# A memset of one element in a run of four indirect gathers, and gathers asked for two groups further on, in a message-passing kernel on one Trainium2 core

## The chip, the cores and the metric

The kernel runs on one core of one Trainium2 chip. The metric is device time in microseconds of one execution; the median of several runs is compared. One further execution was taken by the hardware profiler, and every row of a profile below is from such an execution.

## The reference

A graph has 6250 nodes of 128 features and 100000 edges, sorted by destination. For each edge the features of its source and of its destination go through three layers; the messages are averaged at the destination; a node update with a residual and a layer norm follows.

```python
msg_in = jnp.concatenate([node_features[row], node_features[col]], axis=-1)
h = jax.nn.relu(msg_in @ Wm1 + bm1)
h = jax.nn.relu(h @ Wm2 + bm2)
messages = h @ Wm3 + bm3
agg = jax.ops.segment_sum(messages, col, num_segments=num_nodes)
...
agg = agg / jnp.clip(count, 1.0)[:, None]
node_in = jnp.concatenate([node_features, agg], axis=-1)
upd = jax.nn.relu(node_in @ Wn1 + bn1) @ Wn2 + bn2
return node_features + upd
```

## The kernel before

The first layer is split by its two inputs. In a prologue of about 45 us the kernel turns x, multiplies it by both halves of Wm1 and writes two tables to DRAM: one row of 256 numbers for each node as a source (atab, 1 KB a row) and one for each node as a destination (btab, as three bf16 terms). The edges are then worked through in 196 groups of 512 (four tiles of 128 edges). A group passes these stages:

- Gather (L527 to L536): GpSimd issues four indirect DMAs, one for each tile. Each fetches 128 rows of atab, by 128 indices that lie in SBUF, into one quarter of the tile `rows`. The four are called a run here. Four buffers of `rows` take turns, so the run of group i may only start when the transposes of group i-4 have read that buffer. Groups 0 and 1 take their first layer from other tiles, so group 2 is the first with a run.
- Transposes (`open_layer`, L558 to L572): sixteen products on TensorE turn the gathered rows into PSUM, with the identity as the moving operand. L582 adds the destination's terms by a one-hot product, and ACT adds the bias and cuts at zero (L588).
- Second layer (L596): sixteen fp32 products of 128x256 a group; DVE takes the maximum with the negative bias (L598).
- Sums (L604 to L624): a one-hot product sums the edges of a window of nodes; ACT copies the sums (L609), TensorE turns them (L617) and DVE adds them into an accumulator in SBUF (L624).
- From about the middle on the node update of finished nodes is interleaved.

One loop over steps k (L845 to L920) sets the order: step k does the first layer of group k, asks for a gather, does the second layer of group k-1, and then sums. TensorE, ACT and DVE run in the order in which this code is written. The order on GpSimd and SP is set by a scheduler at build time, from the code and its dependences. In this loop the gather of group k+2 is asked for in step k (L879, L880).

The indices: `sources(g)` (L749) hands a gather its indices. Those of even groups, and of groups up to 4, are read from `srcT` in place. Those of odd groups above 4 are first copied, 128x4 integers, into one of four slots of `srcP`. The copy is made by DVE in every second step for the group five ahead (L893), and for group 5 by ACT in step 2 (L878). Such a gather waits for its copy.

Of the kernel before, what the change touches and what calls it, by code (L numbers as in the profile page):

```python
# [10 lines left out]
F32 = mybir.dt.float32  # L11
# [9 lines left out]
P = 128  # L21
# [8 lines left out]
XS = 1  # L30
B_FIRST = 4
B_EARLY = 8
B_FROM = 10


@with_exitstack
def kernel(
# [36 lines left out]
    nc = tc.nc  # L74
# [4 lines left out]
    GT = 4  # L79
    GE = GT * P  # L80
    HE = 2 * P
    NG = -(-E // GE)
# [27 lines left out]
    const = ctx.enter_context(tc.tile_pool(name="const", bufs=1))  # L110
    dram = ctx.enter_context(tc.tile_pool(name="dram", bufs=1, space=DRAM))

    srcT = const.tile([P, NG, GT], I32, name="srcT")
    srcX = const.tile([P, 2 * XS, GT], I32, name="srcX")
    srcP = const.tile([P, 4, GT], I32, name="srcP")
# [19 lines left out]
    nc.vector.memset(idle, 0.0)  # L135
    ident = const.tile([P, P], F32, name="ident")
    make_identity(nc, ident)
    iota_n = const.tile([P, 1, WN], F32, name="iota_n")
    nc.gpsimd.iota(iota_n, pattern=[[0, 1], [1, WN]], base=0, channel_multiplier=0,
                   allow_small_or_imprecise_dtypes=True)  # L140
# [148 lines left out]
    halves = [slice(h * NQ, (h + 1) * NQ) for h in range(2)]  # L289
# [9 lines left out]
    with tc.tile_pool(name="prep", bufs=1) as prep, tc.tile_pool(name="pp", bufs=3, space=PSUM) as pp, tc.tile_pool(  # L299
        name="pb", bufs=5, space=PSUM  # L300
# [177 lines left out]
        for i in range(BLOCKS):  # L478
            tiles = range(4 * i, min(4 * i + 4, NT), 2)
            rows = a_rows[i % len(a_rows)]  # L480
# [34 lines left out]
    with edge, tc.tile_pool(name="wk", bufs=2) as wk, tc.tile_pool(  # L515
        name="banks", bufs=7, space=PSUM
# [7 lines left out]
        def bank():  # L524
            return banks.tile([P, 2, H], F32, name="bank")
# [1 line left out]
        def flat_bank():  # L527
            return bank().rearrange("p t h -> p (t h)")

        def gather(idx):  # L530
            ag = ld.tile([P, GT, H], F32, name="rows")
            for j in range(GT):
                nc.gpsimd.indirect_dma_start(  # L533
                    out=ag[:, j, :], out_offset=None, in_=atab[:, :],
                    in_offset=bass.IndirectOffsetOnAxis(ap=idx[:, j:j + 1], axis=0))
            return ag  # L536
# [21 lines left out]
        def open_layer(ag, nt, xt=None):  # L558
            nh = nt // 2
            ph = [bank() for _ in range(nh)]  # L560
            for c in range(HC):
                if xt is not None:
                    for h in range(nh):
                        nc.tensor.matmul(ph[h][:, c, :], w1[:, 0, c * P:(c + 1) * P], xt[:, h * HE:(h + 1) * HE],
                                         start=(c == 0), stop=False, skip_group_check=True)
                    continue
                for u in range(GT):
                    for h in range(nh):
                        nc.tensor.matmul(ph[h][:, c, u * NQ:(u + 1) * NQ], ag[halves[h], u, c * P:(c + 1) * P],  # L569
                                         ident[halves[h], halves[h]], is_transpose=True,  # L570
                                         start=(c == 0 and u == 0), stop=False, skip_group_check=True)
            return ph  # L572

# [63 lines left out]
        def nk_of(g):  # L637
            return 1 if g < 2 * HALVES or g >= GL else 2
# [108 lines left out]
            nc.sync.dma_start(rows_of(out, k), y[:r, :n, :])  # L747

        def sources(g):  # L749
            return srcP[:, g % 4, :] if g > 4 and g % 2 else srcT[:, g, :]  # L750

        def pace(g):
            return srcP[:, g % 4, :], srcT[:, g, :]
# [26 lines left out]

        B_STEPS = B_FROM + 2 * (NT - B_EARLY) + 2
        begins, step = {}, B_STEPS
# [5 lines left out]
        nodes, terms, rows = [], {}, {}  # L788
# [58 lines left out]
        def next_rows():  # L847
            for last in (False, True):
                for parts in next_four:
                    b_term(*parts, last)  # L850
# [6 lines left out]
        for g in range(-4, NG + 14, 2):  # L857
# [10 lines left out]
            for k in (g, g + 1):  # L868
                if k < NG:
                    s = st[k] = {}  # L870
                    if k == 1:
                        xts[1] = open_layer(None, NTS[1], xts[1])
                    s["h1"] = first_layer(rows.pop(k, None), terms.pop(k), ohts[k // 2][:, k % 2], NTS[k], nk_of(k),
                                          xts.pop(k, None))
                    if k == 0:
                        next_rows()
                    if k == 2:
                        nc.scalar.copy(*pace(5))  # L878
                if 2 * XS <= k + 2 < NG:  # L879
                    rows[k + 2] = gather(sources(k + 2))  # L880
                if k % 2 == 0 and k + 2 < NG:
                    make_hot(k // 2 + 1)
                if 0 <= k - 1 < NG:
                    second_layer(st.pop(k - 1)["h1"], h2s[(k - 1) % len(h2s)], NTS[k - 1])
                if k < NG:
                    node_step(k)
                if k <= NG:
                    turn_sums(k)
                some_sums(k)
                if k > NG:  # L890
                    turn_sums(k)
                if k % 2 == 0 and 2 <= k and k + 5 < NG:
                    nc.vector.tensor_copy(*pace(k + 5))  # L893
                if k >= NG:
                    node_step(k)
            if g < 6:
                clear(8)
            if g == 0:
                more_rows()
            t0 = B_EARLY + (g - B_FROM) // 2  # L900
            if g >= B_FROM and (g - B_FROM) % 4 == 0 and t0 < NT:
                pbt = bank()
# [21 lines left out]
        with tc.If(again > 0, preferred_fallthrough_block=True, label="again"):  # L924
            with tc.For_i(0, NG, 1) as g:
# [13 lines left out]
                with tc.For_i(0, more, 1):  # L939
                    idx = wk.tile([P, GT], I32, name="idx")  # L940
# [52 lines left out]
```

## Time and profile before

| | us |
|---|---|
| median of 3 runs | 1339.38 |
| lowest and highest run | 1335.79, 1342.36 |
| profiled execution, its time | 1338.36 |
| profiled execution, span from first to last instruction | 1336.6 |
| TensorE products busy | 1236.1 (92%) |
| TensorE weight loads busy (beside products) | 925.5 (69%) |
| GpSimd busy | 748.7 (56%) |
| DVE busy | 618.2 (46%) |
| ACT busy | 441.9 (33%) |
| granted TensorE clock, mean over the span | 0.981 |

In the rows of the profile PE is TensorE, PEld its weight loads, POOL GpSimd, DVE VectorE, ACT ScalarE, SP SyncE. A row of a time-line has the start and the length in us, the engine, the line of the kernel, what is written and read, how many alike follow each other, and in brackets the idle time of the engine just before and what ended it; "issue" means that nothing which the profile shows was waited for. A row of groups has the busy time in us, the mean length of one in ns, and the idle time before all of them. On GpSimd a gather's length is that of issuing it; its data moves afterwards.

### The profile page before, as it was taken

What the parts mean: (1) busy time and instruction counts of PE and PEld (TensorE: products, weight loads), DVE (VectorE), ACT (ScalarE), POOL (GpSimd) and SP (SyncE); (2) the same over time, 40 slices, a digit from 0 to 9 for tenths busy, and PEclk for the clock granted to TensorE, in tenths of its full rate; (3) what the DMA queues carried; (4) which work ended last, traced back from release to release, by engine and by line L of the source; (5) the groups of instructions that cost most, each with busy time, mean ns of one, the idle gap of its engine ahead of it and who ended that gap; (6) DMA issues with size and microseconds to landing.
All of it is one profiled execution on the core that took longest, in us unless ns stands there. A gap on an engine that the chain in (4) does not pass through costs nothing.

```text
span 1336.6 us, 27771 instructions
## 1 busy us (share of the span) xinstructions
PE 1236.1 (92%) x10031; PEld 925.5 (69%) x10032; DVE 618.2 (46%) x1551; ACT 441.9 (33%) x1102; POOL 748.7 (56%) x795
## 2 busy tenths in 40 slices
PE   9779998998999999999899999999999999999997
PEld 7556666666666666676677777777777777777675
DVE  6443333433334333434466554444445556556553
ACT  4432323323323323333333423333233333333331
POOL 2366665665665666656555465565655555555550
PEclk9879999999999999999999999999999999999998
DMA  8544434444434434434444344444444434443330
GB/s 287 177 125 134 132 108 127 130 115 129 133 106 128 135 107 125 134 106 131 126 118 119 114 125 128 118 120 129 118 118 118 115 109 118 109 123 110 106 91 4
DMA packets 107617, 163.90 MB, mean 123 GB/s; under 512 B 26367, under 2 KB 71549, under 8 KB 107457
## 3 DMA queue, kind: packets, MB, share of 16 engines
q0 software_dynamic: 37504, 102.29, 27.7%
q1 hardware_dynamic: 69425, 59.50, 14.0%
q8 instruction: 82, 1.34, 0.4%
q14 instruction: 62, 0.51, 0.1%
q10 hardware_dynamic: 544, 0.26, 0.1%
HBM read 142.48 MB, written 19.86 MB: 121 GB/s over the span
## 4 chain that ended last, share of the span: by engine, by line
PE 89%; issue 7%; DVE 2%; another core or an unknown queue 1%; DMA 1%; ACT 0%; SPq 0%; DVEq 0%
PE bank L596 54%; PE bank L569 9%; PE sum_bank L604 9%; PE bank L582 4%; PE bank L617 2%; PE pbt L431 2%; PE bank L727 2%; PE bank L700 2%; PE bank L719 2%; PE bank L715 2%; PE bank L904 1%; PE pt L448 0%; DVE acc L660 0%; DVE x_sb L598 0%
## 5 line engine op out<-in xcount | busy, mean ns | idle before, releaser
L596 PE MATMUL bank<-w,h 128*128 128x256 f32 x3128 | 768.7, 392 | 67.2 <-issue 64.6
L596 PEld LDWEIGHTS bank<-w,h 128*128 128x128 f32 x3128 | 581.7, 192 | 212.3 <-issue 131.1
L533 POOL DMA_INDIRECT rows<-atab,srcT x392 | 374.9, 956 | 260.6 <-issue 90.4
L533 POOL DMA_INDIRECT rows<-atab,srcP x384 | 364.2, 949 | 277.9 <-issue 126.5
L588 ACT ACTIVATE h<-bank,b 128x256 f32<-128x256 f32 x782 | 306.5, 476 | 395.6 <-remote 189.3
L598 DVE TENSOR_TENSOR x_sb<-bank,nb 128x512 f32<-128x512 f32 x263 | 181.0, 691 | 401.7 <-PE bank L596 233.7
L598 DVE TENSOR_TENSOR h_more<-bank,nb 128x512 f32<-128x512 f32 x128 | 88.3, 692 | 177.5 <-PE bank L596 75.0
L569 PEld LDWEIGHTS bank<-ident,rows 64*128 64x128 f32 x3096 | 112.7, 140 | 77.7 <-issue 56.8
L569 PE MATMUL bank<-ident,rows 64*128 64x64 f32 x3096 | 139.3, 230 | 0.0
L624 DVE TENSOR_TENSOR acc<-acc,bank 128x96 f32 x382 | 96.7, 253 | 51.7 <-PE bank L569 16.5
L604 PE MATMUL sum_bank<-x_sb,oh 128*32 128x257 f32 x1044 | 104.1, 393 | 3.0 <-issue 1.6
L609 ACT COPY part<-sum_bank 128x257 f32<-128x257 f32 x96 | 35.8, 373 | 197.0 <-PE bank L582 75.4
L582 PE MATMUL bank<-oht,terms 64*128 64x128 bf16 (+1 forms) x1132 | 82.6, 237 | 14.5 <-issue 10.9
L604 PE MATMUL sum_bank<-h_more,oh 128*32 128x257 f32 x512 | 59.1, 391 | 1.2 <-DVE h_more L598 0.6
L604 PEld LDWEIGHTS sum_bank<-x_sb,oh 128*32 128x32 f32 x1044 | 28.1, 108 | 41.7 <-issue 34.1
L582 PEld LDWEIGHTS <-terms 64*128 64x128 bf16 x1132 | 44.1, 97 | 16.1 <-issue 13.8
L617 PE MATMUL bank<-ident,part 128*128 128x128 f32 (+1 forms) x291 | 47.3, 271 | 0.5 <-ACT part L609 0.5
L745 ACT ACTIVATE y<-y,sh,rs 128x128 f32<-128x128 f32 (+3 forms) x50 | 22.1, 487 | 67.0 <-DVE sh L743 26.6
L695 DVE RECIPROCAL x_sb<-x_sb 128x256 f32<-128x256 f32 (+3 forms) x26 | 43.0, 1655 | 0.9
L617 PEld LDWEIGHTS bank<-ident,part 128*128 128x128 f32 (+1 forms) x291 | 36.6, 139 | 9.3 <-ACT part L609 1.0
L552 DVE TENSOR_TENSOR oh<-iota_n,dloc 128x256 f32<-128x256 f32 x98 | 40.8, 417 | 3.6 <-ACT dloc L838 3.6
L737 ACT ACTIVATE sd<-mv,eps 128x2 f32<-128x2 f32 (+3 forms) x26 | 7.7, 295 | 97.6 <-DVE mv L735 49.5
(157 smaller groups left out, 625.0 us busy)
## 6 DMA issues: line engine op xcount, KB each, us to landing
terms<-btab SPq DMA_DIRECT2D x566, 32.0 KB
places<-reltab SPq DMA_DIRECT2D x98, 128.0 KB
btab<-x_sb SPq DMA_DIRECT2D x10, 768.0 KB
rows<-atab,srcT POOLq DMA_INDIRECT x392
atab<-acc SPq DMA_DIRECT2D x12, 512.0 KB
rows<-atab,srcP POOLq DMA_INDIRECT x384
xr<-in_x_dram SPq DMA_DIRECT2D x23, 128.0 KB
out_dram<-y SPq DMA_DIRECT2D x23, 128.0 KB
```

The source lines that it names most:

```text
L533: nc.gpsimd.indirect_dma_start(out=ag[:, j, :], out_offset=None, in_=atab[:, :], in_offset=bass.IndirectOffsetOnAxis(ap=idx[:, j:j + 1], a ...
L552: nc.vector.tensor_tensor(oh[:, :ng].rearrange("p g j n -> p (g j) n"), iota.to_broadcast([P, ng * GT, WN]), dl.rearrange("p (j o) -> p j ...
L569: nc.tensor.matmul(ph[h][:, c, u * NQ:(u + 1) * NQ], ag[halves[h], u, c * P:(c + 1) * P], ident[halves[h], halves[h]], is_transpose=True, ...
L582: nc.tensor.matmul(ph[h][:, c, k * n:(k + 1) * n], bw[halves[h], k, c * P:(c + 1) * P], oht[halves[h], k * n:(k + 1) * n], start=False, st ...
L588: nc.scalar.activation(h1[:, c, h * HE:(h + 1) * HE], ph[h][:, c, :], AF.Relu, bias=b1[:, c:c + 1])
L596: nc.tensor.matmul(ph2[:, j - j0, :], h1[:, c, j * P:(j + 1) * P], w2[:, c, :], start=(c == 0), stop=(c == HC - 1))
L598: nc.vector.tensor_tensor(h2[:, j0:j0 + 2, :H], ph2, nb2.to_broadcast([P, 2, H]), op=ALU.max)
L604: nc.tensor.matmul(pg[w * WN:(w + 1) * WN, :H + 1], oh, h2, start=(t == 0), stop=(t == total - 1), skip_group_check=True)
L609: nc.scalar.copy(part[:nw * WN], pg[:nw * WN, :H + 1])
L617: nc.tensor.matmul(pt[:, c, :q], rows, ident[:q, :q], is_transpose=True, start=True, stop=True, skip_group_check=True)
L624: nc.vector.tensor_add(window, window, pt[:, :, j * WN:(j + 1) * WN])
L695: nc.vector.reciprocal(rc, rc)
```

## The change

1. A second tile `turner`, 128x128, is filled in the prologue by a copy of the identity on DVE. The sixteen transposes of a group read it in place of the identity; all other users keep the identity.
2. For groups from 20 on the source has, between the second and the third gather of a run, a memset on GpSimd that writes 1.0 to the one element [0, 0] of `turner`, which is 1.0 already.
3. Step k asks for the gather of group k+4 in place of k+2; steps 0 and 1 ask for two groups each (2 and 3, 4 and 5).
4. Group 5's indices are read in place, and the copy of ACT is gone; copied indices begin with group 7.

```diff
+GATED = 20
...
     ident = const.tile([P, P], F32, name="ident")
     make_identity(nc, ident)
+    turner = const.tile([P, P], F32, name="turner")
+    nc.vector.tensor_copy(turner, ident)
...
-        def gather(idx):
+        def gather(idx, gated=False):
             ag = ld.tile([P, GT, H], F32, name="rows")
             for j in range(GT):
+                if gated and j == GT // 2:
+                    nc.gpsimd.memset(turner[0:1, 0:1], 1.0)
                 nc.gpsimd.indirect_dma_start(
...
                         nc.tensor.matmul(ph[h][:, c, u * NQ:(u + 1) * NQ], ag[halves[h], u, c * P:(c + 1) * P],
-                                         ident[halves[h], halves[h]], is_transpose=True,
+                                         turner[halves[h], halves[h]], is_transpose=True,
...
-            return srcP[:, g % 4, :] if g > 4 and g % 2 else srcT[:, g, :]
+            return srcP[:, g % 4, :] if g > 6 and g % 2 else srcT[:, g, :]
...
-                    if k == 2:
-                        nc.scalar.copy(*pace(5))
-                if 2 * XS <= k + 2 < NG:
-                    rows[k + 2] = gather(sources(k + 2))
+                for i in (range(2 * XS + 2 * k, 2 * XS + 2 * k + 2) if k < 2 else (k + 4,)):
+                    if i < NG:
+                        rows[i] = gather(sources(i), GATED <= i)
```

What stands in the engines' queues, as built. In these rows DMA is one gather of a run, and the brackets name the engines or queues whose signals a row waits for: DMASW those of earlier gathers, PE TensorE, DVE, Activation and Pool the engines of that name. GpSimd from the last gather of group 19's run on, before:

```order
L533 DMA rows<-atab,srcP 128x256 [waits DMASW7_49]
L533 DMA rows<-atab,srcT 128x256 [waits DMASW0_49,PE_49]
L533 DMA rows<-atab,srcT 128x256 [waits DMASW1_49]
L533 DMA rows<-atab,srcT 128x256 [waits DMASW2_49]
L533 DMA rows<-atab,srcT 128x256 [waits DMASW3_49]
L533 DMA rows<-atab,srcP 128x256 [waits DMASW4_49,DVE_49,PE_49]
```

The same place after:

```order
L538 DMA rows<-atab,srcP 128x256 [waits DMASW7_49]
L537 MEMSET turner 1x1 [waits PE_49]
L538 DMA rows<-atab,srcT 128x256 [waits DMASW0_49,PE_49]
L538 DMA rows<-atab,srcT 128x256 [waits DMASW1_49]
L538 DMA rows<-atab,srcT 128x256 [waits DMASW2_49]
L538 DMA rows<-atab,srcT 128x256 [waits DMASW3_49]
L537 MEMSET turner 1x1 [waits PE_49,Pool_49]
L538 DMA rows<-atab,srcP 128x256 [waits DMASW4_49,DVE_49,PE_49]
```

The scheduler put the memset ahead of the first gather of its run; so it stands in all 176 runs that have one. It waits for TensorE, for the transposes of group i-4. No gather changed its place among the gathers.

TensorE at the transposes of group 17, before:

```order
L604 MATMUL sum_bank<-x_sb,oh 32x257 [waits DVE_49]
L569 MATMUL bank<-ident,rows 128x64 [waits DMASW4_49,PE_49]
L569 MATMUL bank<-ident,rows 128x64 [waits PE_49]
L569 MATMUL bank<-ident,rows 128x64 [waits DMASW5_49]
L569 MATMUL bank<-ident,rows 128x64
```

The same place after:

```order
L609 MATMUL sum_bank<-x_sb,oh 32x257 [waits DVE_49]
L574 MATMUL bank<-turner,rows 128x64 [waits DMASW4_49,Pool_49]
L574 MATMUL bank<-turner,rows 128x64 [waits PE_49]
L574 MATMUL bank<-turner,rows 128x64 [waits DMASW5_49]
L574 MATMUL bank<-turner,rows 128x64
```

TensorE's products stand as before; the first transpose of a group now waits for GpSimd in place of TensorE's own earlier work, for the memset of the group three later.

GpSimd at the run of group 5, with the row ahead of it and the row behind it, before:

```order
L533 DMA rows<-atab,srcT 128x256 [waits DMASW3_49]
L533 DMA rows<-atab,srcP 128x256 [waits DMASW4_49,Activation_49]
L533 DMA rows<-atab,srcP 128x256 [waits DMASW5_49]
L533 DMA rows<-atab,srcP 128x256 [waits DMASW6_49]
L533 DMA rows<-atab,srcP 128x256 [waits DMASW7_49]
L533 DMA rows<-atab,srcT 128x256 [waits DMASW0_49,PE_49]
```

The same place after:

```order
L538 DMA rows<-atab,srcT 128x256 [waits DMASW3_49]
L538 DMA rows<-atab,srcT 128x256 [waits DMASW4_49]
L538 DMA rows<-atab,srcT 128x256 [waits DMASW5_49]
L538 DMA rows<-atab,srcT 128x256 [waits DMASW6_49]
L538 DMA rows<-atab,srcT 128x256 [waits DMASW7_49]
L538 DMA rows<-atab,srcT 128x256 [waits DMASW0_49,PE_49]
```

Group 5's run waits only for the landing of earlier gathers; the run of group 6 behind it waits for TensorE, as before. On DVE the copy of the identity (L140) stands between the copy into `iota_b` and the memset of `iota_b`, in the prologue; on ACT one copy is gone; SP is unchanged.

## The prediction

> **What bounds the kernel now.** I read the page first (busy times and the costliest groups), then the time-line of GpSimd in the middle of the kernel, then all engines over the same stretch, then the first 100 us.
>
> ```profile
> span 1336.6 us, 27771 instructions
> PE 1236.1 (92%) x10031; PEld 925.5 (69%) x10032; DVE 618.2 (46%) x1551; ACT 441.9 (33%) x1102; POOL 748.7 (56%) x795
> ...
> L596 PE MATMUL bank<-w,h 128*128 128x256 f32 x3128 | 768.7, 392 | 67.2 <-issue 64.6
> ...
> L533 POOL DMA_INDIRECT rows<-atab,srcT x392 | 374.9, 956 | 260.6 <-issue 90.4
> L533 POOL DMA_INDIRECT rows<-atab,srcP x384 | 364.2, 949 | 277.9 <-issue 126.5
> ```
>
> TensorE is busy for 92% of the span, GpSimd for 56%, and nearly all of that is gathers (374.9 + 364.2 of 748.7 us). TensorE's products of the second layer have 67.2 us of idle time ahead of them, 64.6 of it put down to "issue", so to no producer. GpSimd idles 538.5 us ahead of its gathers. So what the change adds on GpSimd lies on an engine with room, if the room is where the addition falls. The time-line of GpSimd (start, duration, idle before it and who ended it) shows that:
>
> ```profile
> 601.35 0.94 POOL L533 DMA_INDIRECT rows<-atab,srcP  x1 [1.34 <-remote]
> 602.59 0.94 POOL L533 DMA_INDIRECT rows<-atab,srcP  x1 [0.30 <-issue]
> 603.84 0.95 POOL L533 DMA_INDIRECT rows<-atab,srcP  x1 [0.30 <-issue]
> 605.09 0.95 POOL L533 DMA_INDIRECT rows<-atab,srcP  x1 [0.30 <-issue]
> 607.45 0.95 POOL L533 DMA_INDIRECT rows<-atab,srcT  x1 [1.42 <-PE bank L596]
> ...
> 613.62 0.95 POOL L533 DMA_INDIRECT rows<-atab,srcP  x1 [1.32 <-PE bank L617]
> ...
> 620.04 0.94 POOL L533 DMA_INDIRECT rows<-atab,srcT  x1 [1.72 <-PE bank L596]
> ...
> 626.26 0.94 POOL L533 DMA_INDIRECT rows<-atab,srcP  x1 [1.52 <-PE bank L596]
> ```
>
> A run of four gathers takes 4.69 us (601.35 to 606.04), 0.30 us apart, then GpSimd waits 1.3 to 1.7 us for a signal of TensorE, and the next run starts 6.1 to 6.4 us after the one before. The other engines at two of those starts:
>
> ```profile
> 613.49 1.57 ACT L588 ACTIVATE h<-bank,b 128x256 f32<-128x256 f32 x4 [3.49 <-PE bank L596]
> 613.56 1.41 DVE L598 TENSOR_TENSOR h_more<-bank,nb 128x512 f32<-128x512 f32 x2 [3.26 <-PE bank L617]
> 613.62 0.95 POOL L533 DMA_INDIRECT rows<-atab,srcP  x1 [1.32 <-PE bank L617]
> 614.01 0.71 PE L569 MATMUL bank<-ident,rows 64*128 64x64 f32 x16
> ...
> 621.97 0.71 PE L569 MATMUL bank<-ident,rows 64*128 64x64 f32 x16
> ```
>
> ACT, DVE and GpSimd are let go within 0.13 us of each other: TensorE's signals arrive in a bunch, between two runs. The transposes of a group follow the start of a run by 0.39 us at 614.01 and 1.93 us at 621.97 (after 620.04). What ends last in a step is TensorE's own work and, in light steps, that bunch of signals; the gathered rows are there long before.
>
> **The change part by part.** First, where the memset goes. By GpSimd's order around group 20, shown with the change, the memset stands ahead of the first gather, not between the second and the third as the source has it: the runs of four stay whole. It waits for the transposes of four groups earlier, and so did the gather behind it, for its buffer. So the wait is not new; the memset's own time is, 176 times (groups 20 to 195). Asking two groups further on changes no gather's place: GpSimd's row holds nothing but gathers, and the four buffers hold each to the same transposes.
>
> No row shows a 1x1 memset. The nearest, by groups, and the nearest copy on DVE to the added one of the identity:
>
> ```profile
> masks.py:197 POOL MEMSET ident<- 128x128 f32 x1 | 0.2, 204 | 0.3 <-POOLq L979 0.3
> ...
> L979 POOL MEMSET const-float32-0.0<- 128x1 f32 x1 | 0.1, 99 | 0.1
> ...
> 8.78 0.42 DVE L453 COPY xT<-pt 128x256 f32<-128x256 f32 x1
> ```
>
> A memset costs between 0.10 us (128x1, the nearer) and 0.20 + 0.30 = 0.50 us (128x128, with the step between GpSimd's instructions); I take 0.15, so 26 us of GpSimd's 538.5 idle ones. They fall at the end of a wait, so the run starts and ends later by 0.15. Does the next one start later too? Two runs in which a gather took longer answer that:
>
> ```profile
> 97.03 0.94 POOL L533 DMA_INDIRECT rows<-atab,srcT  x1 [1.62 <-PE bank L582]
> 98.28 1.71 POOL L533 DMA_INDIRECT rows<-atab,srcT  x1 [0.30 <-issue]
> ...
> 103.39 0.94 POOL L533 DMA_INDIRECT rows<-atab,srcP  x1 [0.89 <-PE bank L582]
> ```
>
> ```profile
> 582.97 0.94 POOL L533 DMA_INDIRECT rows<-atab,srcT  x1 [1.57 <-PE bank L582]
> ...
> 585.47 1.21 POOL L533 DMA_INDIRECT rows<-atab,srcT  x1 [0.30 <-issue]
> ...
> 589.11 0.94 POOL L533 DMA_INDIRECT rows<-atab,srcP  x1 [1.17 <-PE bank L596]
> ```
>
> The run at 582.97 ends at 587.94 (589.11 less 1.17), 4.97 us long, 0.28 over 4.69; the next starts 6.14 us after it, 0.04 over the 6.10 from 601.35 to 607.45. The wait gave way, and a seventh of the delay came through. At 97.03 it is 0.78 us longer (103.39 less 0.89 less 97.03, less 4.69) and the next start 6.36, 0.26 over: a third. For a delay as small as a memset I take the seventh: 176 x 0.15 / 7 = +3.8 us, with ends of 0 (all of it hidden in TensorE's own work) and, by the third, 176 x 0.15 / 3 = +8.8.
>
> [...]
>
> TensorE's side gets a wait: the transposes now read what the memset writes. By its order, shown at group 17, its work stays where it was; the first transpose of group k waits for the memset of group k+3, which stands behind run k+2 on GpSimd and behind the transposes of group k-1. Queued behind it on TensorE are the group's sixteen transposes, the B terms and the second layer of the group before. The margin is the 0.39 and 1.93 us above. A memset of 0.10 to 0.20 us is over by then, so I take 0; at 0.50 us the smaller margin is passed by 0.11, and if every second group were like it that is 88 x 0.11 = +9.7 us.
>
> The copy of the identity stands on DVE between its first small operations in the prologue, ahead of the index work for which the first gathers wait: between 0 and 0.42 us (half of that row's size, so I take +0.2). No other row of DVE moves.
>
> Last, groups 2 to 6. Group 5 no longer reads the paced copy of its indices. By GpSimd's order there, shown with the change, the wait for ACT is gone, so the first sixteen gathers follow each other. What that meets, by the time-line of the early part (GpSimd, ACT's copy, TensorE):
>
> ```profile
> 45.62 0.94 POOL L533 DMA_INDIRECT rows<-atab,srcT  x1 [25.44 <-DMA terms<-btab]
> ...
> 59.67 0.95 POOL L533 DMA_INDIRECT rows<-atab,srcT  x1 [0.30 <-issue]
> ...
> 63.08 3.57 PE L596 MATMUL bank<-w,h 128*128 128x256 f32 x8 [0.84 <-issue]
> ...
> 64.79 0.21 ACT L878 COPY srcP<-srcT 128x4 int32<-128x4 int32 x1
> 65.27 0.94 POOL L533 DMA_INDIRECT rows<-atab,srcP  x1 [4.65 <-ACT srcP L878]
> ...
> 68.02 3.72 PE L596 MATMUL bank<-w,h 128*128 128x256 f32 x16
> ...
> 72.93 0.47 PE L596 MATMUL bank<-w,h 128*128 128x256 f32 x1 [0.33 <-issue]
> ...
> 79.67 0.95 POOL L533 DMA_INDIRECT rows<-atab,srcP  x1 [0.30 <-issue]
> ...
> 82.46 3.63 PE L596 MATMUL bank<-w,h 128*128 128x256 f32 x7 [1.17 <-issue]
> ```
>
> Twelve gathers in a burst (45.62 to 60.62), a wait of 4.65 us for the copy, and twelve more (65.27 to 80.62). In each burst TensorE slows to a matmul at a time, "issue" ahead of each, and is at its pace again about 2 us after its end (63.08, 82.46). With four more gathers at 1.25 us (0.95 + 0.30) the first burst ends 5.0 us later, and so I expect TensorE at its pace: +5.0. The second burst then falls apart, for group 6 must wait for the transposes of group 2 and group 7 for those of group 3, which come only when TensorE is let go. Its slow stretch, nine products from 72.93 to 82.46, takes 9.53 us where the row at 68.02 gives 9 x 3.72 / 16 = 2.1: -7.4. The sum is -2.4 us; the ends are -7.4 (the first stretch no longer) and +5.0 (the second stays).
>
> **The sum** is +3.8 + 0 + 0.2 - 2.4 = +1.6 us, on the profiled execution's 1338.36 us (1336.6 of span and 1.76 around it): 1340.0. The median of the runs shown is 1.02 us above that execution, so the forecast is 1341.0 us. One measurement of this kernel can tell about 0.5% from no change, 6.7 us; the ends of the terms give 1338.36 + 1.02 - 7.4 = 1332 to 1339.4 + 8.8 + 0.4 - 2.4 = 1346.
>
> **The rivals.** (A) Slower: TensorE's signals come out only once a run has landed, so run, landing and the next start form one loop, and the memset is part of it. For it speaks that starts follow a run's end at nearly one distance (1.32, 1.42, 1.52) and that three engines are let go at once; against it, the two long runs, after which the wait shrank to 1.17 and 0.89. Its price is the memset's whole time in each of 176 steps: 0.15 x 176 = 26 us, so 1339.4 + 26 - 2.4 = 1363, from 1355 (0.10) to 1425 (0.50). It decides if the wait after a run stays at 1.3 us or more while the run starts later.
>
> (B) Faster: the second early stretch goes with all that hangs on it. The windows (length, busy time and number per engine, then the granted clock) show that TensorE ran at half its clock around both bursts:
>
> ```profile
> 58.00:68.00 10.00, 6.67 (x31) 4.50 (x31) 4.41 (x8) 1.65 (x5) 4.43 (x5) 0.50 0.38 128
> ...
> 78.00:92.00 14.00, 9.98 (x41) 5.47 (x42) 5.29 (x10) 2.61 (x7) 6.97 (x9) 0.51 0.27 79
> ```
>
> If TensorE is not starved a second time, the clock is not halved from 78 to 92 us, and of 9.98 busy us up to half, 5.0, goes too: -2.4 - 5.0 = -7.4 on top of nothing lost later, 1332.0; with the first stretch no longer than before, -12.4, 1327. For it: both half-clock stretches begin inside a burst. Against: the first is likely to grow by as much as the second shrinks. [...]
>
> (C) The early bursts join and the second stays: +5.0, 1344.4, no change that can be measured.
>
> (D) A run broken in the middle would let signals out earlier; by the order no run is broken, so I give it nothing of its own.
>
> **How the numbers follow.** Forecast 0.56, A 0.26, B 0.14, C 0.04. Forecast and C are within 0.5%: same 0.60; A is slower, 0.26; B faster, 0.14. A gets a quarter since the evidence against it is two runs; B less, since it needs both early effects to fall well. The forecast's own range is 1332 to 1346. The range of 1330 to 1360 takes it in, reaches into B as far as 9 us and into A as far as a memset of 0.13 us, about half of A; it leaves out some 0.06 of B and 0.13 of A.
>
> **What would show it.** In the changed profile: 176 memsets of 0.1 to 0.2 us, each ahead of a run's first gather; runs still 4.69 us long with 0.30 between gathers; the wait ahead of memset and run together still 1.3 to 1.7 us at starts 6.1 to 6.4 us apart; no idle time of TensorE of any size put down to GpSimd ahead of the transposes; sixteen gathers from 45.6 to 65.6 us, TensorE at its pace near 68, and no slow stretch from 73 to 82. I am wrong if starts are further apart by the memset's time (A), if the transposes wait for GpSimd, if memsets take 0.5 us or more, or if the early part alone moves the end by over 6 us.

## The result, and the profile after

| | before | after |
|---|---|---|
| median, us | 1340.87 (4 runs, 1335.79 to 1348.21) | 1420.78 (4 runs, 1413.10 to 1424.49) |
| profiled execution, its time | 1338.36 | 1424.49 |
| its span | 1336.6 | 1422.7 |
| granted TensorE clock, mean | 0.981 | 0.943 |

The changed kernel is slower: the ratio of its time to that of before is 1.0579, with a 95% interval of 1.0544 to 1.0615. I had forecast 1341 us and a range up to 1360. The page of the changed kernel, the busy times and the groups that answer to those of before:

```profile
span 1422.7 us, 28175 instructions
...
PE 1278.5 (90%) x10031; PEld 963.9 (68%) x10032; DVE 613.9 (43%) x1552; ACT 440.6 (31%) x1101; POOL 765.3 (54%) x971
...
L601 PE MATMUL bank<-w,h 128*128 128x256 f32 x3128 | 787.2, 403 | 45.2 <-issue 42.5
...
L538 POOL DMA_INDIRECT rows<-atab,srcT x396 | 379.3, 958 | 186.3 <-issue 102.2
L538 POOL DMA_INDIRECT rows<-atab,srcP x380 | 360.8, 949 | 166.0 <-issue 96.6
...
L574 PE MATMUL bank<-turner,rows 64*128 64x64 f32 x3096 | 161.1, 234 | 63.6 <-issue 62.3
...
L537 POOL MEMSET turner<- 1x1 f32 x176 | 15.7, 89 | 256.3 <-PE bank L574 85.0
```

The memsets themselves are short: 176 of 89 ns, 15.7 us. The gathers cost what they did. The work of TensorE is the same, yet its busy time is 42.4 us more (1278.5 less 1236.1) and its idle time 43.7 us more (the rest of the 86.1 by which the span grew). Of its idle time 63.6 us sit in a new place, at the transposes (0.0 before), put down to "issue" and not to GpSimd; the second layer's fell from 67.2 to 45.2 us. Where the step got longer shows the time-line of GpSimd, ACT and the transposes:

```profile
603.23 0.71 PE L574 MATMUL bank<-turner,rows 64*128 64x64 f32 x16
603.57 0.95 POOL L538 DMA_INDIRECT rows<-atab,srcT  x1 [0.30 <-issue]
603.78 0.38 PE L587 MATMUL bank<-oht,terms 64*128 64x256 bf16 x4
...
605.83 0.09 POOL L537 MEMSET turner<- 1x1 f32 x1 [1.31 <-remote]
606.00 1.57 ACT L593 ACTIVATE h<-bank,b 128x256 f32<-128x256 f32 x4 [2.27 <-remote]
...
606.57 0.94 POOL L538 DMA_INDIRECT rows<-atab,srcP  x1 [0.66 <-PE bank L601]
```

The run before ends at 604.52, and TensorE's signals come out together 1.3 us later, as before the change. But now the memset takes them, at 605.83, and the first gather starts 0.74 us after the memset did (606.57), with the 0.66 us idle between them. Before, the first gather itself started with the signals (613.62, next to ACT at 613.49). Over the kernel, the first and last starts of a run with a memset, and of the same two runs before:

```profile
L537 POOL MEMSET turner<- x176: 88/88/221, 154.7 to 1378.5; 1x1 f32 x176
```

```profile
158.80 0.94 POOL L533 DMA_INDIRECT rows<-atab,srcT  x1 [1.37 <-PE bank L596]
...
1293.22 0.94 POOL L533 DMA_INDIRECT rows<-atab,srcP  x1 [2.33 <-PE bank L582]
```

175 steps take 1223.8 us after and 1134.4 before: 6.99 and 6.48 us each, 0.51 us more, 89.4 in all. That is the whole loss and 3.3 us over it, for what came ahead of group 20 ended earlier. The rows above are no exception: by the time-line of GpSimd, which gives 175 of the 176 memsets, a memset starts 1.46 us (median) after the end of the run before, where before the change the first gather started 1.55 us after it, and the gather starts 0.72 us after its memset. In means the wait shrank from 1.75 to 1.46 us and the 0.76 us from memset to gather came on top; a run itself is 0.04 us longer.

### The profile page after: what moved, and what is told of

Same layout as the page of the kernel before. It is cut to its first block, busy times and chain, and to the rows that moved or that the text cites. A ratio compares the mean times of both kernels' runs of the same rounds, so it can differ in the third digit from the quotient of the medians.

```text
span 1422.7 us, 28175 instructions
## 1 busy us (share of the span) xinstructions
PE 1278.5 (90%) x10031; PEld 963.9 (68%) x10032; DVE 613.9 (43%) x1552; ACT 440.6 (31%) x1101; POOL 765.3 (54%) x971
## 4 chain that ended last, share of the span: by engine, by line
PE 85%; issue 9%; another core or an unknown queue 1%; DVE 1%; DMA 1%; POOL 1%; ACT 0%; SPq 0%; DVEq 0%; POOLq 0%; ACTq 0%
PE bank L601 52%; PE bank L574 10%; PE sum_bank L609 8%; PE bank L587 4%; PE bank L622 2%; PE bank L732 2%; PE bank L705 2%; PE pbt L434 2%; PE bank L724 1%; PE bank L720 1%; PE bank L908 1%; POOL rows L538 1%; DMA x_sb<-in_x_dram 1%; DVE x_sb L603 0%
## 5 line engine op out<-in xcount | busy, mean ns | idle before, releaser
L601 PE MATMUL bank<-w,h 128*128 128x256 f32 x3128 | 787.2, 403 | 45.2 <-issue 42.5
L601 PEld LDWEIGHTS bank<-w,h 128*128 128x128 f32 x3128 | 607.4, 200 | 185.8 <-issue 88.3
L538 POOL DMA_INDIRECT rows<-atab,srcT x396 | 379.3, 958 | 186.3 <-issue 102.2
L574 PEld LDWEIGHTS bank<-turner,rows 64*128 64x128 f32 x3096 | 124.2, 142 | 149.3 <-issue 144.4
L574 PE MATMUL bank<-turner,rows 64*128 64x64 f32 x3096 | 161.1, 234 | 63.6 <-issue 62.3
L537 POOL MEMSET turner<- 1x1 f32 x176 | 15.7, 89 | 256.3 <-PE bank L574 85.0
L587 PE MATMUL bank<-oht,terms 64*128 64x128 bf16 (+1 forms) x1132 | 86.7, 247 | 11.9 <-issue 10.0
```

What stands on the lines that cost most here:

```text
L538: nc.gpsimd.indirect_dma_start(out=ag[:, j, :], out_offset=None, in_=atab[:, :], in_offset=bass.IndirectOffsetOnAxis(ap=idx[:, j:j + 1], a ...
L587: nc.tensor.matmul(ph[h][:, c, k * n:(k + 1) * n], bw[halves[h], k, c * P:(c + 1) * P], oht[halves[h], k * n:(k + 1) * n], start=False, st ...
L601: nc.tensor.matmul(ph2[:, j - j0, :], h1[:, c, j * P:(j + 1) * P], w2[:, c, :], start=(c == 0), stop=(c == HC - 1))
```

## The experiments

Theory A is rival (A) of the prediction with another price: GpSimd's runs, the landing and TensorE's signals form a cycle, and what stands between the signals and a run's first gather lengthens it, here by about 0.7 us. Theory T is its rival: TensorE loses the time at its transposes, which now wait for a memset on GpSimd. The kernels were run in groups, each beside the kernel before on one chip. The time of the kernel before differed between the groups (1190, 1321, 1323, 1341 and 1341 us), so ratios are compared.

**First group (before: 1189.97 us).** No memsets (`GATED = 1000`):

> The changed kernel without its 176 memsets: the copy of the identity, the gathers asked for two groups further on and the unpaced group 5 stay. If the memsets cost the whole loss (82 us), this runs at the time of the kernel before less the early saving seen in the two profiles (run 20 starts at 155.4 us and not at 158.8): 1334 to 1340 us. If asking further on or reading another tile than the identity costs part of it, it stays above 1347 us.

The memset in a pad of the rows buffer, which nothing reads:

```diff
-            ag = ld.tile([P, GT, H], F32, name="rows")
+            wide = ld.tile([P, GT * H + 8], F32, name="rows")
+            ag = wide[:, :GT * H].rearrange("p (j h) -> p j h", j=GT)
             for j in range(GT):
-                if gated and j == GT // 2:
-                    nc.gpsimd.memset(turner[0:1, 0:1], 1.0)
+                if gated and j == 0:
+                    nc.gpsimd.memset(wide[0:1, GT * H:GT * H + 1], 1.0)
```

> The memset writes an unused element at the end of the rows buffer, ahead of the run's first gather. It waits for the same transposes of four groups earlier, by the buffer, but TensorE waits for no memset. Theory A (GpSimd's start is delayed: the memset is let go by the bunch of signals and the first gather starts 0.72 us after it, in a loop of run, landing and signals): as slow as the changed kernel, 1395 to 1430 us, runs 6.9 us apart. Theory T (TensorE loses the time waiting at its transposes for the memset): 1334 to 1342 us. If the first gather, which here has no wait of its own for TensorE, follows the memset at 0.30 us, the 0.72 was that second wait, and the time lies between, near 1370 us.

Three copies of the identity in turn (gather i writes copy i % 3, the transposes of group k read copy k % 3):

> Three copies of the identity take turns, so that a memset waits for transposes six groups back, done long before, and not four; the transposes still wait for the memset of three groups ahead, which stands behind the run before it on GpSimd. Theory A: the memset fits into the wait after a run and the first gather starts as in the kernel before: 1334 to 1345 us. Theory T: TensorE is still held by GpSimd: 1390 to 1425 us.

The order of GpSimd's code kept, so that the memset really stands between the second and the third gather:

```diff
-        turns.enter_context(tc.manual_schedule(engines={ENG.Activation, ENG.DVE}))
+        turns.enter_context(tc.manual_schedule(engines={ENG.Activation, ENG.DVE, ENG.Pool}))
```

> GpSimd in the order of the code, so that the memset stands between the second and the third gather, as the source has it. Theory A: it waits for nothing there and fits between two gathers (0.09 us in the 0.30), runs stay 4.7 to 4.8 us long and start as before; the only cost is TensorE waiting for the middle of the run three groups ahead, 2.5 us after its start, which by the rows of the kernel before (transposes 0.39 and 1.93 us after a run's start) holds some of the groups: 1340 to 1370 us. Theory T: the later memset holds TensorE longer than in the changed kernel: above 1425 us.

Measured: 1190.33 us, ratio 1.0000 (0.9991 to 1.0010); 1190.48, 1.0004 (0.9994 to 1.0013); 1189.50, 0.9995 (0.9985 to 1.0005); 1201.02, 1.0091 (1.0074 to 1.0108). Nothing of A or T could be told apart, for in this group the kernel before took 11% less than in the result. Only the memset between two gathers cost something, 11 us; its trace shows TensorE waiting 8.0 us for that memset, 7.4 of them at one place. The profile of the kernel without memsets shows a different picture from the one before:

```profile
PE 1173.0 (99%) x10031; PEld 915.0 (77%) x10032; DVE 614.6 (52%) x1552; ACT 441.0 (37%) x1101; POOL 755.3 (64%) x795
```

```profile
502.80 0.38 PE L587 MATMUL bank<-oht,terms 64*128 64x256 bf16 x4
...
503.26 0.99 POOL L538 DMA_INDIRECT rows<-atab,srcT  x1 [0.40 <-PE bank L587]
503.27 1.57 ACT L593 ACTIVATE h<-bank,b 128x256 f32<-128x256 f32 x4 [3.84 <-PE bank L587]
```

TensorE is busy for 99%. ACT starts 0.47 us after the start of the products that it waits for, though a run is just under way; in the rows above it was 606.00 less 603.78, 2.2 us, and only once the run was over. Signals were prompt here, and GpSimd had time to spare. The time-lines from 180 to 1280 us say the same of the whole: here ACT's activations start 0.48 us (median) after the start of these products, and 149 of their 187 rows begin inside a run; in the profile before it is 2.57 us, and 163 of 185 begin between two runs.

**Second group (before: 1320.69 us): the changed kernel again, and with memsets from group 108 only.**

> The changed kernel once more, beside the kernel before on one chip. In the first group of experiments the kernel before took 1190 us, where it took 1340 in the comparison of the result, and in the profiles TensorE's signals reach ACT 0.5 us after the work and not after 4 us. Theory A': the memset costs time only where those signals come late, so that GpSimd's runs bound the step: on a chip where the kernel before takes 1190 us the changed kernel takes 1190 to 1196 us; where it takes 1340, 1413 to 1425. Rival T (TensorE is held at its transposes by the memset): slower by 60 us or more on either.

> The memsets only from group 108 on, 88 in place of 176. Where the changed kernel loses 82 us, theory A (so much for each memset) gives half of it less the early saving: 38 to 45 us over the kernel before; if a few joined bursts early on made the loss, it is nearly nothing or nearly all. Where the kernel before takes 1190 us: no change.

Measured: 1402.20 us, ratio 1.0606 (1.0562 to 1.0649), and 1354.78, 1.0242 (1.0202 to 1.0282). Half of the memsets cost 34 us (I had expected 38 to 45), all of them 82 us: the loss goes about with their number, and it is not made at one place. That the changed kernel costs nothing where signals are prompt was not tried with the changed kernel itself; the pad and the three copies, which also put a memset ahead of a first gather, cost nothing there.

**Third group (before: 1323.03 us): the first four kernels again.**

> Without the memsets, again, to have it where TensorE's signals come late. Where the kernel before takes 1320 to 1340 us: if the memsets are the whole loss, 0 to 5 us below the kernel before; if asking two groups further on costs part, at least 10 us above it. Where it takes 1190 us: the same time, as in the first group.

> The memset in an unused element of the rows buffer, again. Where the kernel before takes 1320 to 1340 us: theory A (GpSimd's start is delayed by 0.66 to 0.72 us in a loop of run, landing and signals) gives 60 to 85 us over the kernel before, runs 6.8 to 6.9 us apart; theory T (TensorE held by the memset at its transposes) gives 0 to 5 us below it. Where it takes 1190 us: the same.

> Three copies of the identity in turn, again, so that the memset waits for nothing new, while TensorE's transposes still wait for it. Where the kernel before takes 1320 to 1340 us: theory A gives a time within 10 us of the kernel before, if the memset runs right behind the run before and the first gather still waits for the signals by itself; if the 0.66 us is paid whenever a memset stands ahead of a gather, waited for or not, 60 us or more over. Theory T gives 60 to 80 us over, with idle time of TensorE ahead of its transposes.

> The memset between the second and third gather, as the source has it, again. Where the kernel before takes 1320 to 1340 us: it costs GpSimd nothing, for it falls into the 0.30 us between two gathers, so theory A gives no more than the 11 us over the kernel before that the first group showed, by TensorE's wait for the middle of a run; theory T gives more than the changed kernel, over 80 us.

Measured: without memsets 1320.99 us, 0.9994 (0.9968 to 1.0019); pad 1392.98, 1.0557 (1.0506 to 1.0607); three copies 1402.41, 1.0617 (1.0575 to 1.0659); between 1321.95, 1.0001 (0.9978 to 1.0023). The memsets are the whole loss. A memset that TensorE never waits for costs as much as the one that it waits for, to within the intervals, so T falls. GpSimd with the pad:

```profile
603.95 0.09 POOL L538 MEMSET rows<- 1x1 f32 x1 [1.23 <-PE bank L602]
604.61 0.95 POOL L539 DMA_INDIRECT rows<-atab,srcT  x1 [0.57 <-issue]
```

Here the gather has no wait of its own for TensorE, and it still starts 0.66 us after the memset: the 0.57 us behind the memset, which the profile puts down to "issue", are not a second wait for TensorE. The three copies did not do what I meant: the scheduler moved each memset two runs further ahead, so that it stood ahead of another run's first gather and waited for the same signals. It is one more case for A, and not the one that I had set up. The memset between two gathers:

```profile
603.26 0.94 POOL L538 DMA_INDIRECT rows<-atab,srcP  x1 [0.30 <-issue]
604.20 0.09 POOL L537 MEMSET turner<- 1x1 f32 x1
604.51 0.95 POOL L538 DMA_INDIRECT rows<-atab,srcP  x1 [0.21 <-issue]
...
608.62 0.95 POOL L538 DMA_INDIRECT rows<-atab,srcT  x1 [1.91 <-remote]
```

It lies wholly within the 0.30 us that stood there anyway. The same kernel's waits of TensorE:

```profile
PE bank L574 <- POOL turner L537: 32.2, 51, 2.1
PE bank L601 <- issue: 24.5, 49, 1.9
```

TensorE does wait for this memset, 32.2 us in 51 places, and loses nothing by it: the second layer's "issue" idle is 24.5 us instead of the 55.5 without memsets in this group (64.6 in the profile before).

**Fourth group (before: 1341.15 us).** The memset behind the fourth gather, three memsets ahead of the first, a pause in the middle, and group 5 paced again. In the pause, in place of the memset of `turner`:

```diff
+                    for _ in range(5):
+                        nc.gpsimd.memset(idle, 0.0)
```

> GpSimd in the order of the code, with the memset behind the fourth gather of its run. It waits for nothing, and the next run's first gather stands at the head of GpSimd's queue while it waits for TensorE's signals, as in the kernel before. Theory A2 (a first gather that is already in hand starts at once when the signals come, and one that stands behind a waiting instruction starts 0.57 us after it): 0 to 10 us over the kernel before, with the first gather right at the signals. Rival F (any memset between two runs costs 0.6 us, waited for or not): 60 us or more over.

> GpSimd in the order of the code, three memsets of one element ahead of the first gather in place of one. Theory A2: the first waits and the others follow at 0.1 us each, and the start of the gather stays 0.57 us behind the last: 0.2 us more a step, 25 to 40 us over the loss of the changed kernel, 105 to 120 us over the kernel before. If each instruction on GpSimd costs 0.66 us in front of a gather: 230 us more. If the gather is being set up while the memsets run: no more than the changed kernel's loss of 80 us.

> GpSimd in the order of the code, and between the second and third gather five memsets of a tile that nothing reads any more (128 partitions), 0.2 us or more each, so that GpSimd issues no gather for 1 us or more in the middle of a run; no memset is read by TensorE. This leaves the element of the identity alone. If TensorE's signals are held back as long as GpSimd issues gathers, they come out in this pause: ACT's activations (L594) start in the middle of a run, and the time is 0 to 30 us over the kernel before or below it. If they are held back until a run's data has landed, however it is spread, each step grows by the pause: 1.0 us x 176, 150 us or more over.

> No memsets, and group 5 reads its indices from the paced copy again, made by ACT in step 0. Together with the run without memsets this prices the first sixteen gathers in one burst. My prediction's early term gives 2.4 us over the time without memsets; within 3 us of it either way the term can't be told from nothing.

Measured: behind 1367.76 us, 1.0195 (1.0134 to 1.0257); three 1425.50, 1.0617 (1.0555 to 1.0679); pause 1367.50, 1.0194 (1.0135 to 1.0253); paced 1343.38, 1.0008 (0.9981 to 1.0036). Behind the run:

```profile
601.84 0.09 POOL L540 MEMSET turner<- 1x1 f32 x1
601.98 0.71 PE L574 MATMUL bank<-turner,rows 64*128 64x64 f32 x16 [1.15 <-POOL turner L540]
...
603.09 1.57 ACT L593 ACTIVATE h<-bank,b 128x256 f32<-128x256 f32 x4 [1.82 <-PE bank L587]
603.22 0.94 POOL L536 DMA_INDIRECT rows<-atab,srcP  x1 [1.30 <-PE bank L587]
```

The first gather is back at the signals (603.22, ACT at 603.09): a memset that waits for nothing, with the gather at the head of the queue, delays no run, and F falls. But this kernel lost 26 us, more than the 10 I allowed, and by theory T's way: the transposes now wait for the end of a run.

```profile
PE bank L574 <- POOL turner L540: 73.8, 80, 2.5
```

So T's wait is real where the memset is late; it is not what made the changed kernel slow. That the wait makes the 26 us is argued and not shown, since the memset between two gathers had 32.2 us of it at no cost. With three memsets:

```profile
608.85 0.38 POOL L537 MEMSET turner<- 1x1 f32 x3 [1.67 <-remote]
609.85 0.94 POOL L538 DMA_INDIRECT rows<-atab,srcT  x1 [0.61 <-issue]
```

The gather starts 1.00 us after the first memset, 0.26 later than with one, as A2 says; but the time is no more than the changed kernel's ratio. My 25 to 40 us did not come, and the expectation under which three cost as much as one came true in its number, though not by its reason, since the gather does start later. Over all its runs the gather starts 1.07 us after the first memset in the mean, 0.31 later than with one, but the wait ahead of the memsets is 1.18 us in place of 1.46, so the steps are 7.01 us where they were 6.99: of the further delay nearly nothing came through. A possible reason is that even when the signals are there early, three memsets leave a break of 1.02 us between two runs (601.47 to 602.49 in this profile), while in the changed kernel such runs follow each other with no more than the usual 0.30 us. I did not test it. TensorE beside such a row of eight gathers in the changed kernel:

```profile
618.63 0.09 POOL L537 MEMSET turner<- 1x1 f32 x1
618.93 0.95 POOL L538 DMA_INDIRECT rows<-atab,srcP  x1 [0.21 <-issue]
...
621.15 0.29 PE L574 MATMUL bank<-turner,rows 64*128 64x64 f32 x2 [0.25 <-issue]
621.43 0.94 POOL L538 DMA_INDIRECT rows<-atab,srcP  x1 [0.30 <-issue]
622.60 0.26 PE L574 MATMUL bank<-turner,rows 64*128 64x64 f32 x1 [1.15 <-issue]
...
624.71 0.38 PE L574 MATMUL bank<-turner,rows 64*128 64x64 f32 x2 [1.14 <-issue]
625.43 0.74 PE L574 MATMUL bank<-turner,rows 64*128 64x64 f32 x9 [0.34 <-issue]
```

The memset was let go at once at 618.63, eight gathers follow each other (from 613.93 on), and TensorE crawls through the transposes at a product in 0.7 to 1.4 us, and is at its pace again 1.8 us after their end (623.62). About 40 of the 62.3 us of "issue" at the transposes fall into such rows of eight. They are not needed for the loss: with three memsets no eight gathers follow each other without a break, the transposes still have 48.7 us of "issue", and the loss is the same.

The pause shows when the signals come out. In the middle of a run GpSimd issues no gather for 1.8 us:

```profile
608.86 1.80 POOL L538 MEMSET idle<- 128x256 bf16 x5
...
610.36 0.39 PE L588 MATMUL bank<-oht,terms 64*128 64x256 bf16 x4
610.82 1.01 POOL L539 DMA_INDIRECT rows<-atab,srcP  x1 [0.15 <-issue]
610.84 1.57 ACT L594 ACTIVATE h<-bank,b 128x256 f32<-128x256 f32 x4 [5.53 <-PE bank L588]
...
615.59 1.80 POOL L538 MEMSET idle<- 128x256 bf16 x5
616.83 1.57 ACT L594 ACTIVATE h<-bank,b 128x256 f32<-128x256 f32 x4 [1.41 <-PE bank L588]
...
620.07 0.95 POOL L539 DMA_INDIRECT rows<-atab,srcP  x1 [0.30 <-PE bank L623]
```

ACT now starts in the middle of a run, 1.24 us into the second pause, and the next run joins without a wait (0.30): here the signals came out in a pause of the gathers, with half of a run still to be issued. Whether the issuing of gathers or the moving of their data, which goes on after it, holds the signals is not told apart by this (in the profile before, the last gather is issued by 1297.92 us, and the gathers' queue still moves 0.13 MB between then and 1300). The step is now four gathers, 5.0 us, and the pause. The 175 steps are 6.71 us in the mean, 39 us more than before in all; the span grew by 27.8 us (1364.4), for the kernel ends 33 us after the start of its last run, where it was 43.

The paced group 5 tested nothing of the early burst: its copy was ready in time, and sixteen gathers still follow each other (group 5's first at 62.57 us with 0.31 us of idle). It stands as a second run without memsets.

**Fifth group (before: 1340.74 us): shorter pauses.** Four memsets, three, and four in all runs (`GATED = 2`):

> As with five memsets in the middle of a run, with four: the pause is 1.45 us by 0.36 us each, and a run with its pause and the next run behind it 6.32 us (6.68 less 0.36). If TensorE's signals still come out in the pause (ACT's activations began 1.2 to 2.0 us after the pause of 1.81 did), the steps go from 6.48 us to about 6.35: 15 to 30 us below the kernel before where it takes 1320 us or more; where it takes 1190 us, TensorE was busy for 99% at steps of 5.8 us, so steps of 6.3 us there are slower by 90 us. If the pause is too short for the signals, the joined runs starve TensorE: over 100 us slower.

> With three memsets the pause is 1.1 us and a run 5.96 us. The earliest signals came 1.2 us into a pause. If they need that long, some come late by a whole run and TensorE stalls: slower than with four by 20 us or more. If 1.1 us is enough, TensorE bounds the step again (6.3 us at its share of 92% before): 20 to 50 us below the kernel before where that takes 1320 us or more.

> Four memsets in every run from the first on, so that the burst of the first sixteen gathers is broken as well. TensorE's crawl from 53 to 67 us in the changed kernel should go: up to 8 us below the run with four memsets from group 20 on, less what the pauses of the first runs cost (4 x 1.45 us before the rows of group 5 land); if the crawl stays, the same or 5 us slower.

Measured: four 1340.29 us, 0.9991 (0.9961 to 1.0022); three 1356.94, 1.0095 (1.0064 to 1.0126); four in all runs 1341.87, 1.0008 (0.9982 to 1.0034). Four memsets, so 1.44 us, give the time of before and no gain; with three, 1.07 us, the kernel takes 17 us more than with four. I had said 20 or more if that is too short for the signals; that it is too short is read from the time alone. GpSimd and TensorE's waits with four:

```profile
606.20 1.43 POOL L538 MEMSET idle<- 128x256 bf16 x4
607.79 0.95 POOL L539 DMA_INDIRECT rows<-atab,srcT  x1 [0.16 <-issue]
...
612.50 1.44 POOL L538 MEMSET idle<- 128x256 bf16 x4
```

```profile
PE bank L602 <- issue: 30.1, 48, 2.2
PE bank L575 <- issue: 23.5, 41, 1.4
PE bank L588 <- issue: 10.1, 20, 1.2
```

The step shown is 6.30 us (606.20 to 612.50), near the expected length, and it is the usual one (median 6.31). But 28 of the 176 runs still wait for more than 0.5 us, and in the mean a step is 6.50 us (the runs of group 20 and of the last group start at 158.12 and 1296.38), as long as the 6.48 of before. TensorE's idle "issue" is spread over three groups (63.7 us) and is about what it was at the second layer before (64.6). My 15 to 30 us were wrong: the cycle on GpSimd became shorter in most steps, but not over the kernel. In the last kernel the early crawl is gone (sixteen products of the second layer at 49.48 us in 3.72 us, and again at 55.34, where the changed kernel's came one at a time from 56.35 to 67.00); but the sixteenth gather then starts at 70.19 us, where in the changed kernel it was 63.03, and nothing is gained. No version here beats the kernel before.

## Why the prediction was wrong

- Where the memset goes: right. It stood ahead of the first gather, all 176 times, and the run stayed whole.
- What the memset costs: this step failed. I priced it by its own time, 0.10 to 0.50 us with 0.15 as the likely value. Its own time was 0.09 us, but the price was the time from its start to the gather's, 0.66 to 0.74 us in the rows above. I had taken the step of 0.30 us between two instructions on GpSimd as the most that could stand behind it; that row is of a gather behind a gather. A gather that stood at the head of the queue, waiting, had started with the signal (0.13 us after ACT, at 613.62 before and again at 603.22 with the memset behind the run); in the rows above 0.57 to 0.66 us of idle time stand between a memset that had waited and the gather behind it.
- How much of a delay comes through: this step failed as well. I took a seventh, from two runs that were longer because a gather in them took longer. The step grew by 0.51 us for a delay of 0.76 in the mean, so two thirds. The seventh was also a thin reading: it is 0.04 us over a single step of 6.10, while the steps in the rows beside it go from 6.10 to 6.42. Those two runs were delayed inside, by a gather that took longer, while no other was issued, and in the pause experiment signals came out 1.24 us after the gathers had stopped; so they may have been no measure of a delay at a run's head. That this is why they differ is argued, not shown, and the three memsets, whose further 0.31 us came through hardly at all, show that no fixed share holds.
- The range: the upper end of 1346 took the memset at 0.15 us and left out the +9.7 of the transposes' wait and the +5.0 of the early part. With the prediction's own 0.50 us and a third (176 x 0.50 / 3 = 29) and these two, it would have reached 1384, still below the 1421 measured.
- The rival on the other side, (A), named the right cycle, but for the landing: by the pause, signals come out with half a run still to be issued. At its price, 0.74 us by 176 is 130 us; 89 came. That its span of 1355 to 1425 takes in the 1421 measured is luck: that end is a memset that itself lasts 0.50 us and comes through whole. The point from which I said that it decides (the wait after a run stays at 1.3 us while the run starts later) is what the profile shows: 1.31 us ahead of the memset at 605.83. I gave it 0.26, and its weight against the two long runs was misjudged.
- TensorE's wait at the transposes, priced at 0: right for this place of the memset, by the pad that costs the same without it. Behind a run the same wait has a price of 26 us.
- The early part, -2.4 us: the burst of sixteen, TensorE at its pace at 67.00 us (expected near 68) and no slow stretch from 73 to 82 us all came (the granted clock from 78 to 92 us was 1.00, and 0.51 before); group 20's run starts 3.4 us earlier in the profile (155.4 and 158.8), but 1.7 us of that is there at the first gather already (43.97 and 45.62), which no term had. In the times it can't be told from nothing: 0.9994 (0.9968 to 1.0019) without memsets.

```profile
64.90 0.58 PE L601 MATMUL bank<-w,h 128*128 128x256 f32 x1 [2.31 <-issue]
67.00 3.63 PE L601 MATMUL bank<-w,h 128*128 128x256 f32 x7 [1.51 <-issue]
```

- The copy of the identity: 207 ns on DVE, as taken. The six memsets of the changed kernel that ran beside an index copy on DVE took 0.09 us like the others. One of the 176 took 0.22 us; it ran beside another DVE instruction and ended 0.03 us after it. Why it took longer is not shown:

```profile
715.15 0.29 DVE L699 TENSOR_SCALAR x_sb<-acc 128x256 f32<-128x256 f32 x1
715.25 0.22 POOL L537 MEMSET turner<- 1x1 f32 x1 [3.46 <-PE bank L574]
```

- The clock: its mean fell from 0.981 to 0.943, and the busy time of the same 10031 products rose from 1236.1 to 1278.5 us. In the crawl shown above the granted clock was 1.00 up to 622 us, 0.50 from 623 to 629, though TensorE was busy throughout from 626 on, and 1.00 again from 630. Ahead of the halving TensorE was busy for 0.26 to 0.29 of each us (621 to 623). What sets it is not shown, and what part of the loss is the clock's was not measured.

## What to carry to other kernels

Price an instruction put in front of an asynchronous one by the distance from its start to the start of what stands behind it, and not by its own length, and take that distance from a place where the engine had been waiting. Look at the queue as built: where TensorE's signals came late, the same memset cost about 80 us ahead of the run's first gather, nothing between two gathers and 26 us behind them. A delay that a wait takes up at one place of a cycle need not be taken up at another (of a longer gather inside a run a seventh and a third came through before, of the memset at its head two thirds); ask what ends that wait, and whether it moves along.

## What the runs showed of the hardware

- While GpSimd issued indirect gathers one behind the other, signals of TensorE mostly stayed out: in the profile before ACT started 2.57 us (median) after the start of the products that it waited for, 163 times of 185 between two runs, mostly 1.2 to 1.8 us after the run's end; with a pause put into the run they came out in its middle too, 1.24 us after gathers had stopped. In one group of runs signals were prompt (0.48 us, the kernel without memsets), and there the kernel before took 1190 us, where it took 1321 to 1341 in the others. What sets the one or the other was not found; it is not the chip alone, for the first and the fourth group (1190 and 1341 us) are on record with the same one.
- Where signals came late, TensorE was slowed to a product every 0.7 to 1.4 us beside eight gathers in a row (621 to 625 us of the changed kernel); the trace puts it down to no engine.
- A memset of one element on GpSimd took 88 to 91 ns in the changed kernel and with the pad (one of the 352 took 221), and it fitted into the 0.30 us between two gathers (604.20 to 604.51 us with the memset there); behind one that had waited, a gather took another 0.57 to 0.66 us to start in the rows above.
